# Expert 7 of the first part: single tiles between the experts of the second part, in place of one group of three ahead of the last

## The chip, the cores and the metric

The kernel runs on one core of one Trainium2 chip. Its time is the device time in microseconds (us); of several runs the median is given. Before the change it is 1835.74 us, the median of three runs between 1833.97 and 1839.69.

The core has a matrix engine (PE, whose weight loads are listed as PEld), a vector engine (DVE), a scalar engine (ACT), a general engine (POOL) and a queue engine that only issues transfers (SP). Transfers (DMAs) are issued by SP and by POOL, and run on 16 DMA engines that both share.

## The reference

Four layers follow one another on `x` of shape 16 x 256 x 256, all in 32-bit floats: a cross-attention with eight heads, a feed-forward layer with per-batch weight terms, a second cross-attention, and a mixture of eight experts. Only the last one matters here (cut; `_routing_weights` gives each token a weight for each expert, zero for most):

```python
def _L1_ffn_ref(x, Wg, Wu, Wd, Wr, temperature):
    weights = _routing_weights(x, Wr, temperature)
    gate = jnp.einsum('btd,edi->beti', x, Wg)
    up = jnp.einsum('btd,edi->beti', x, Wu)
    h = jax.nn.silu(gate) * up
    e_out = jnp.einsum('beti,eid->betd', h, Wd)
    out = jnp.einsum('bte,betd->btd', weights, e_out)
    return out
...
x = x + _L1_ffn_ref(_layernorm(x, axis=-1), L1_ffn_Wg, L1_ffn_Wu, L1_ffn_Wd, L1_ffn_Wr, L1_ffn_temperature)
```

Each of the eight experts has 256 inputs, 256 hidden values and 256 outputs. A token's output is the sum over the experts of weight times expert output, added to the token's `x`.

## The kernel before

**Attention and routing.** The main loop runs over 16 batches times 8 heads. Beside it, jobs in a list called `line` fill the gaps of PE: for every batch a job `chain` (the layers up to the second attention) and a job `route`. `route` works out the routing weights and writes each token's row (256 normalised values, eight weights and the token's number, `ROW` is 265 floats) into a slot of each expert that serves it. The slots lie in device memory, in `slots_d`, one array for each of two parts: the first part is batches 0 to 9 (`PARTS = (10, 6)`), the second is batches 10 to 15. The write is an indirect DMA issued by POOL (line 720), 16 for a batch. An expert's slots of the first part that are worked on are ten tiles of 128 rows, of the second part six tiles (`CAPS`).

**Experts.** The job `experts` works through a list of groups `G`. A group is one to four consecutive tiles of one expert and one part. For a group:

- `load` (line 1139) brings its rows from `slots_d` into a buffer `rows`, of which there are two. A read of a part's slots waits until all writes into this part have landed.
- `send_rows` transposes the rows in blocks of 32 on DVE (`to_blocks`, line 291) and sends them to device memory, the "hop" (line 296). `fetch_rows` copies token numbers and weights into `at` and `wt` (`take`, lines 1155 and 1158, six buffers each) and brings the hop back transposed, as `yTd` (`from_blocks`, line 302), in four DMAs. `yTd` has two buffers. All of these DMAs are issued by SP, in the order of the program.
- `gate` and `up` run, for each of two halves `i` of the hidden values, the products `pg` and `pu` over the group's tokens; ACT takes tanh (line 1202), DVE forms `sg` and `hTd` (lines 1212, 1213).
- `down` runs the products `pd` for one tile; DVE scales them by the weight (`o`, line 1228) and POOL adds the rows to `out` by an indirect DMA with addition (line 1229). The down products of a group are put into the program between the gate and up products of the next group.

All matrix products are recorded at line 80, in the helper `mm`. Their outputs share six PSUM buffers (`mm_tile`).

While group n is in work, group n+1 is ready, group n+2 is sent (at `i` = 0) and fetched (at `i` = 1), and the rows of group n+3 are loaded (at `i` = 0). A group of the second part isn't loaded before the routing job of the last batch has been written into the program (`ready`).

**Order of the additions.** Two additions to the same row of `out` must not overlap. `apart` declares that the scatters of one expert and part don't touch each other, and that a scatter of one part doesn't touch those of the other part. So the first scatter of an expert waits until the scatters of the expert before it, in the same part, have landed; scatters of the other part may be issued meanwhile.

**The list.** `groups(part, "", sizes)` makes the groups of each expert with the given numbers of tiles. The list before is: all groups of the first part (4, 3 and 3 tiles for each of experts 0 to 7) but the very last, then experts 0 to 6 of the second part (3 and 3), then the left-out group of expert 7 of the first part (3 tiles), then expert 7 of the second part (3, 2, 1). That makes 41 groups. The weights of an expert, once loaded, stay on the chip.

Of the kernel before, what the change touches and what calls it, by code (L numbers as in the profile page):

```python
# [29 lines left out]
def xattn_ffn_kernel(  # L30
# [16 lines left out]
    E = Wg.shape[0]  # L47
# [692 lines left out]
    with ExitStack() as sh, ExitStack() as sa, ExitStack() as sf:  # L740
# [545 lines left out]
        def groups(part, more, sizes, experts_=range(E)):  # L1286

            gs = []
            for e in experts_:
                t = CAPS[part] // P if more else 0  # L1290
                for k in sizes:
                    gs.append(G(part, e, t, k, more))
                    t += k
                assert t == NTOKS[part] // P if more else t == CAPS[part] // P
            return gs

        first = groups(0, "", (4, 3, 3))
        lists = (  # L1300
            first[:-1] + groups(1, "", (3, 3), range(E - 1))
            + first[-1:] + groups(1, "", (3, 2, 1), [E - 1])
        )

        last = None
        for n in range(NS + 2):
# [102 lines left out]
```

## Time and profile before

| What | Value |
|---|---|
| median of three runs | 1835.74 us |
| time of the profiled execution | 1834.93 us |
| its span | 1833.2 us |
| PE busy | 1805.1 us (98%) |
| DVE busy | 1211.1 us (66%) |
| POOL busy | 850.3 us (46%) |
| ACT busy | 583.9 us (32%) |
| DMA, mean over the span | 181 GB/s |
| granted PE clock, whole run | 0.996 |
| scatters into `out`, line 1229 | 128, mean 1562 ns |

The span is the time from the first to the last instruction of the program in the profiled execution. Busy times are averages over very different stages: in the attention stage POOL is little used, in the last 170 us it is used 60 to 80%. A row of the timeline gives the start of an instruction, its duration, and in brackets the idle time of its engine before it and what ended it. "PE busy" counts a modelled end of each product, and products overlap; the pace of the stage is better read from the starts in the chain of work. DMA rows named SPq are the issues on SP's queue: their duration is that of the issue, not of the transfer.

### The profile page before, as it was taken

The page shows a single profiled execution, that of the slowest core. Times are in us where ns is not written, and L with a number is a line of the kernel's source. Part 1 is how long each engine was busy: PE and PEld are TensorE (multiplying, and loading weights), DVE is VectorE, ACT ScalarE, POOL GpSimd, SP SyncE. Part 2 cuts the span into 40 slices and gives each one's busy share as a digit, 9 for nine tenths or more (in the row PEclk, how much of TensorE's full clock was granted, in tenths as well). Part 3 has the DMA queues.
Part 4 walks back from the last instruction along what each step waited for, and adds up shares of the span by engine and source line. Part 5 has one row for each costly group of instructions (what it writes and reads, how often), then busy time and mean ns, then how long its engine had stood idle before and what let it go on. Part 6 is the DMA issues. An engine that isn't in the chain of part 4 may idle for free.

```text
span 1833.2 us, 22646 instructions
## 1 busy us (share of the span) xinstructions
PE 1805.1 (98%) x6600; PEld 1228.8 (67%) x6600; DVE 1211.1 (66%) x3340; ACT 583.9 (32%) x1299; POOL 850.3 (46%) x988
## 2 busy tenths in 40 slices
PE   8999999999999999999999999999999999999996
PEld 4566666666676666666666666667666777666664
DVE  5456585858585858585858585858575676655553
ACT  3443433333333333334343434333333321111110
POOL 2122235353535353535353535353525267766665
PEclk9999999999999999999999999999999999999998
DMA  6553546464646464646464546554636577999996
GB/s 222 177 184 124 170 138 208 148 197 153 208 149 200 157 203 153 203 149 211 149 204 153 199 156 198 162 196 162 194 125 204 161 215 188 250 246 218 214 211 100
DMA packets 271181, 332.72 MB, mean 181 GB/s; under 512 B 31388, under 2 KB 222792, under 8 KB 271048
## 3 DMA queue, kind: packets, MB, share of 16 engines
q1 hardware_dynamic: 240280, 279.63, 48.4%
q0 software_dynamic: 30720, 51.54, 12.1%
q8 instruction: 55, 0.90, 0.2%
q14 instruction: 78, 0.64, 0.1%
q10 hardware_dynamic: 48, 0.01, 0.0%
HBM read 165.77 MB, written 165.28 MB: 181 GB/s over the span
## 4 chain that ended last, share of the span: by engine, by line
PE 94%; DMA 2%; DVE 2%; POOL 1%; issue 1%; SPq 0%; ACT 0%; DVEq 0%; POOLq 0%; ACTq 0%
PE po L80 13%; PE pv L80 13%; PE sc L80 13%; PE pk L80 12%; PE pq L80 7%; PE px L80 6%; PE pf L80 6%; PE ph L80 6%; PE pg L80 5%; PE pd L80 5%; PE pu L80 5%; PE pl L80 1%; DMA yTd<-hop_rows_b 1%; DMA rows<-slots_d 0%; DVE tb L912 0%
## 5 line engine op out<-in xcount | busy, mean ns | idle before, releaser
L904 POOL TENSOR_SCALAR pr<-pr,ri 128x512 f32<-128x512 f32 x256 | 179.1, 710 | 322.9 <-DVE ri L903 317.9
L896 ACT ACTIVATE pr<-sc,nm 128x512 f32<-128x512 f32 x256 | 173.6, 683 | 478.1 <-DVE nm L890 405.1
L720 POOL DMA_INDIRECT slots_d<-row,at_slot x256 | 253.2, 989 | 70.5 <-issue 69.4
L80 PE MATMUL po<-pT,v 128*128 128x256 f32 x1024 | 242.1, 379 | 1.8 <-DVE W2T L957 1.0
L1229 POOL DMA_INDIRECT out_dram<-o,at x128 | 200.0, 1562 | 92.8 <-issue 23.7
L80 PE MATMUL sc<-kT,qT 128*128 128x512 f32 x512 | 241.0, 593 | 1.5 <-ACT kT L829 1.5
L80 PE MATMUL pk<-kvT,Wk_sb 128*128 128x512 f32 x512 | 240.6, 592 | 0.0
L80 PEld LDWEIGHTS po<-pT,v 128*128 128x128 f32 x1024 | 194.2, 190 | 68.9 <-issue 36.0
L80 PE MATMUL pv<-Wv_sb,kvT 128*128 128x512 f32 x512 | 235.0, 592 | 0.0
L942 DVE TENSOR_SCALAR outT<-po,cvec 128x256 f32<-128x256 f32 x128 | 61.1, 477 | 246.4 <-PE po L80 233.1
L912 DVE STREAM_TRANSPOSE tb<-pr 128x512 f32<-128x512 f32 x256 | 165.8, 686 | 9.2 <-issue 5.0
L80 PEld LDWEIGHTS pv<-Wv_sb,kvT 128*128 128x128 f32 x512 | 97.0, 190 | 108.2 <-issue 103.1
L890 DVE TENSOR_REDUCE nm<-sc 128x1 f32<-128x512 f32 x256 | 160.3, 663 | 2.0 <-PE sc L80 1.9
L80 PEld LDWEIGHTS sc<-kT,qT 128*128 128x128 f32 x512 | 97.0, 190 | 69.9 <-issue 61.2
L80 PEld LDWEIGHTS pk<-kvT,Wk_sb 128*128 128x128 f32 x512 | 97.3, 190 | 67.8 <-issue 61.2
L80 PE MATMUL pq<-kvT,Wq_sb 128*128 128x256 f32 x512 | 133.0, 382 | 0.0
L1202 ACT ACTIVATE sg<-pg 128x384 f32<-128x384 f32 (+3 forms) x82 | 41.3, 503 | 281.3 <-PE pg L80 249.8
L80 PE MATMUL pg<-yTd,wx 128*128 128x384 f32 (+3 forms) x328 | 123.8, 500 | 1.2 <-DMA yTd<-hop_rows_b 0.9
L80 PEld LDWEIGHTS pq<-kvT,Wq_sb 128*128 128x128 f32 x512 | 96.5, 191 | 41.8 <-issue 28.2
L80 PE MATMUL pd<-wx,hTd 128*128 128x256 f32 x512 | 123.9, 379 | 0.2 <-DVE hTd L1213 0.2
L80 PE MATMUL pu<-yTd,wx 128*128 128x384 f32 (+3 forms) x328 | 123.6, 499 | 0.0
L80 PE MATMUL px<-Wo_sb,outT 128*128 128x256 f32 x512 | 121.8, 381 | 0.0
(205 smaller groups left out, 2652.4 us busy)
## 6 DMA issues: line engine op xcount, KB each, us to landing
hop<-tb SPq DMA_DIRECT2D x128, 512.0 KB
pT<-hop SPq DMA_DIRECT2D x512, 128.0 KB
ev<-ev_d SPq DMA_DIRECT2D x32, 512.0 KB
rows<-slots_d SPq DMA_DIRECT2D x31, 397.5 KB
hop_rows_b<-rows_b SPq DMA_DIRECT2D x30, 384.0 KB
yTd<-hop_rows_b SPq DMA_DIRECT2D x120, 96.0 KB
rows<-slots_d SPq DMA_DIRECT2D x8, 530.0 KB
cin<-in_ctx_dram SPq DMA_DIRECT2D x16, 256.0 KB
```

The costliest lines, as they stand in the source:

```text
L80: nc.tensor.matmul(out, lhsT, rhs, **kw)
L720: ins = nc.gpsimd.indirect_dma_start(out=slots_d[part], out_offset=bass.IndirectOffsetOnAxis(ap=at_slot[:, c, e : e + 1], axis=0), in_=row ...
L890: nc.vector.tensor_reduce(nm, sc, AX.X, ALU.max, negate=True)
L896: nc.scalar.activation(pr, sc, AF.Exp, bias=nm, accum_out=sm)
L904: nc.gpsimd.tensor_scalar(pr, pr, ri, 1.0, ALU.mult, ALU.mult)
L912: nc.vector.transpose(tb[:, :, c, :], heads[n][c][0].rearrange("p (m f) -> p m f", m=QP))
L942: nc.vector.tensor_scalar(o, po, col("bv", h), None, ALU.add)
L1202: nc.scalar.activation(self.sg, self.pg, AF.Tanh, scale=0.5)
L1229: ins = nc.gpsimd.indirect_dma_start(out=out_rows[0 : sum(NTOKS[: self.part + 1]), :], out_offset=bass.IndirectOffsetOnAxis(ap=self.at[:, ...
```

## The change

The first part's groups of expert 7 are cut as 3, 1, 1, 1, 1, 1, 1, 1 instead of 4, 3, 3. Its group of three stays behind expert 6 of the first part. The seven single tiles go one by one behind experts 0 to 6 of the second part. Expert 7 of the second part (3, 2, 1) ends the list, as before. The list now has 46 groups; the tiles are the same.

```diff
-        first = groups(0, "", (4, 3, 3))
-        lists = (
-            first[:-1] + groups(1, "", (3, 3), range(E - 1))
-            + first[-1:] + groups(1, "", (3, 2, 1), [E - 1])
-        )
+        first = groups(0, "", (4, 3, 3), range(E - 1)) + groups(0, "", (3,) + (1,) * 7, [E - 1])
+        lists = first[: 1 - E]
+        for e in range(E):
+            lists += groups(1, "", (3, 3) if e < E - 1 else (3, 2, 1), [e])
+            lists += first[1 - E :][e : e + 1]
```

In terms of the last boundary, one tile of the first part now stands ahead of expert 7 of the second part, where three stood. The second part begins after 22 groups instead of 23.

## Prediction

> **What bounds the kernel now.** I read the windows of 20 us over the last stage first, then the chain that ended last, then the engines' timelines there. The windows give busy time of PE, weight loads, DVE, ACT and POOL, the granted clock, the DMA engines' share and GB/s:
>
> ```profile
> 1720.00:1740.00 20.00, 20.00 (x73) 13.67 (x72) 11.84 (x31) 2.45 (x5) 11.98 (x8) 1.00 0.92 212
> 1740.00:1760.00 20.00, 20.00 (x74) 13.85 (x74) 12.40 (x34) 2.46 (x5) 14.25 (x10) 1.00 0.95 199
> ...
> 1800.00:1820.00 20.00, 17.41 (x81) 13.67 (x79) 10.24 (x27) 2.30 (x6) 16.83 (x11) 0.98 0.72 94
> 1820.00:1834.00 14.00, 0.00 (x0) 0.00 (x0) 0.00 (x0) 0.00 (x0) 3.23 (x3) 0.50 0.29 35
> ```
>
> PE never idles until 1817.6, and the DMA engines are over 90% taken. The chain (start, us, work) gives the pace:
>
> ```profile
> 1690.47 1.29 PE pg L80 x4
> 1691.76 1.29 PE pu L80 x4
> 1693.05 1.73 PE pd L80 x8
> 1694.78 1.29 PE pg L80 x4
> ...
> 1812.76 0.44 PE pg L80 x4
> 1813.21 0.45 PE pu L80 x4
> ```
>
> A group of three tiles takes 4 x 1.29 us for gate and up and 3 x 0.86 for the down products of the group before it, 7.75 us, and its successors start at 1698.22, 1705.97, 1713.72, without a hole. The last two lines are the only one-tile group of now. POOL is the other limit. Its timeline (start, us, then idle time before it):
>
> ```profile
> 1728.92 1.54 POOL L1229 DMA_INDIRECT out_dram<-o,at  x1 [0.30 <-issue]
> 1730.77 1.54 POOL L1229 DMA_INDIRECT out_dram<-o,at  x1 [0.31 <-issue]
> 1736.98 1.54 POOL L1229 DMA_INDIRECT out_dram<-o,at  x1 [4.66 <-DVE wt L1158]
> ...
> 1820.45 1.54 POOL L1229 DMA_INDIRECT out_dram<-o,at  x1 [0.30 <-issue]
> 1822.30 1.54 POOL L1229 DMA_INDIRECT out_dram<-o,at  x1 [0.30 <-issue]
> ```
>
> One scatter takes 1.85 us with its gap. Where the next expert of the same part begins, POOL stands 3.1 to 4.7 us: the DVE instruction named had long been done, so it is the landing of the expert before (start to next start is 4.7 to 6.2 us, mean 5.7). Six tiles are 13.9 to 15.5 us on POOL, mean 15.0, against 2 x 7.75 = 15.5 on PE, so POOL hardly catches up: expert 7's first scatter of the first part runs at 1693.85, 17 us after its tile was made, and the last one at 1822.30, 4.2 us after its tile (DVE's last o, 1817.64 to 1818.12). PE and POOL both bound the end, 4 us apart.
>
> **The change.** Tiles, weights, matmul columns and scatters stay the same in number; 41 groups become 46 (expert 7's 4, 3, 3 become 3 and seven ones). Added are 5 row loads, 5 hops and 20 fetches on SP's queue, and five sets of small DVE and ACT instructions.
>
> *PE work.* One-tile gate and up batches take 0.44 to 0.45 us, and a third of 1.29 is 0.43: 7 x 4 x 0.015 = 0.4 us. Against this stands the Trainium skill, "TensorE: Matmul & The Clock Gate", Back-to-back issue gap: in streams of weight load and matmul it measured about 81 ns at 128 columns and 131 at 512, so a short one costs 0.62 of a long one. Scaled to the 0.43 us of a 512-column instruction here (1.72 for four) this estimate is 0.27 us each, 7 x 16 x 0.16 = +18 us. The row is of the same operation in the same stage: I take 0.4.
>
> *POOL.* A single tile of expert 7 may scatter while the second part's landing is awaited: the groups are declared independent, and the crossing from one part to the other shows only 0.30 us of gap at 1706.78. From one boundary to the next POOL still needs 5 x 1.85 + 5.7 = 15.0 us, now for seven tiles, while PE needs 7 x 2.585 = 18.1. Started at 1693.85, it has worked off its lag by the sixth list. The six last scatters then follow their tiles: with o made at 1809.35, 1810.21, 1812.80, 1814.56, 1815.42 and 1817.64, the last starts at 1818.65 instead of 1822.30: **-3.65 us**. More cannot come, since PE's last product stands in front. From here every stall of PE counts in full.
>
> *The start of the second part.* It moves one group of four tiles forward. Its first rows are loaded one group earlier, where SP now issues another row load at 1652.02. But the last scatter into the slots is issued by POOL at 1653.69, and its semaphore reaches its last count at 1659.44. SP stands 7.4 us with the fetch of expert 7's tiles behind it (now at 1657.01; then about 1660.0 to 1661.7, landing near 1665.9 instead of 1664.28): PE +1.5. The rows land 5 to 7 us after 1659.5; DVE's transposes, now at 1659.28, wait in line until about 1665.5, with the o, sg and hTd behind them; the hop leaves at 1666.7, lands at 1670.5, the fetch lands at 1675.5. The second part could have begun at 1664.41 + 7.75 = 1672.16: **+3.4 us**, between 0 (rows landing at once, six PSUM buffers covering DVE) and 6.
>
> *Index buffers.* `at` has six buffers, freed by the landing of scatters six groups back; DVE already waits twice for that, 2.6 us each. Six groups now span 2 x 18.1 = 36 us rather than 46.5, with POOL late. Going through the takes with the start shifted by 3.4, two meet a wait of 1.7 us while PE has PSUM buffers to fill: 0.3, from 0 to 3.
>
> *The prefetch at short groups.* SP's order for a group is hop, next row load, four fetches; a fetch waits for the hop's landing:
>
> ```profile
> 1694.68 0.34 SPq L296 DMA_DIRECT2D hop_rows_b<-rows_b  x1
> 1695.07 0.43 SPq L1139 DMA_DIRECT2D rows<-slots_d  x1
> 1697.78 1.74 SPq L302 DMA_DIRECT2D yTd<-hop_rows_b  x4
> ```
>
> The hop is issued 4.21 us after its group's first gate (1690.47). I took the landings from the semaphores: in the thirteen groups from here to 1790, hop issue to the last fetch's landing took 6.97 to 9.58 us, mean 8.4 (five early ones 9.0, eight later ones 8.0). The data are needed two groups on, 15.5 us after the first gate: 2.9 us spare. Now the groups are 7.75 (second of a list), 4.3 (4 x 0.43 + 3 x 0.86, a single) and 6.0 (first of a list, one down product). A list's first group has 7.75 + 4.3 - 4.21 = 7.86 us: put against the thirteen times, the excess is 0.62 on the mean. Its second group is sent from within the single, about 2.5 us in (1.47 to hTd, 1.05 for three transposes), its rows some 0.35 late, and is needed at 4.3 + 6.0 + 0.6: 2.85 + 8.4 - 10.95 = 0.3, with the spread 0.5. Seven times 0.62 and six times 0.5 are **+7.3 us**. The single itself has some 3.7 us to spare.
>
> Here the skill's price differs: "DMA: Bandwidth & Descriptors", Anatomy of one DMA, sets about 2.0 us plus bytes at 436 GB/s. That makes the hop 2.9 us and the fetch 1.3 of issue plus 2.2, 6.4 in all, under 7.86: no stall, and a sum of about zero. It was fitted for the other issuing path, and the trace's 8.4 was taken with the engines 92 to 95% shared. The trace decides; 0 and 16 us (all at 9.5) are kept as ends.
>
> **Sum** against the profiled execution, 1834.93 us (span 1833.2 and 1.7 around it): 0.4 + 3.4 + 0.3 + 7.3 - 3.65 = +7.75, or 1842.7. The median of the runs, 1835.74, is 0.8 higher, which gives 1843.5; I trim half a microsecond for the relief that stalls give to the DMA engines: **1843 us**.
>
> **Rivals.** (1) *The prefetch keeps up*: landings near 8 us throughout; then 0.4 + 3.4 + 0 to 1 - 3.65, about 1836, and 1832.5 where the start costs nothing either. For it speaks that the later landings are 8.0; against it that even these exceed 7.86. It decides where PE's stalls sum to less than 3.65. This is the case that ends not slower. (2) *Contention grows*: while it works off its lag POOL issues a scatter each 2.14 us instead of 2.5, on engines already over 0.92 taken. At 9.5 us the two stalls are 1.65 and 0.6 in each round: 7 x 2.25 = 16, or 1852. (3) *The single does not pass the wait*: if POOL waited before and after it, a round would be 7 x 1.85 + 2 x 3.9 = 20.7 us where PE has 18.1; the last list would start near 1699.4 + 7 x 20.7 = 1844.3 instead of 1813.05, the end near 1867; the 0.30 at the crossings speaks against it. (4) *Faster by over 0.3%* would need 5.5 us (about what a measurement of this kernel can tell from no change): only 3.65, and 0.95 of an old PE stall at 1664.41, are in sight.
>
> **How the numbers follow.** The forecast 0.50 (its own range 1838 to 1848), (1) 0.27, (2) 0.17, (3) 0.02, (4) 0.04. Slower by over 0.3% is above 1841.2: 0.40 of the forecast's 0.50, (2) and (3), 0.59. Same: 0.10 and most of (1), 0.35. Faster 0.06. The range holds (1) without its start-free end and (2) up to a little beyond its price: 1834 to 1855.
>
> **What would show it.** Right: POOL's gaps at the second part's boundaries near 2 us early and its scatters following their tiles at the end; PE holes before pg, ended by the yTd fetch, at lists' first and second groups, some 1 us a round; SP waiting some 7 us for the slots; PE's last product about 11 us later. Wrong: a gapless PE in the second part, or DVE waits at `at` or `rows` that stop PE for longer than the fetches do.

## The result

The changed kernel takes 1847.63 us (median of four runs, 1846.85 to 1849.13), the kernel before 1837.72 us in the same comparison (1833.97 to 1840.48). The ratio is 1.006, with a 95% interval from 1.0044 to 1.0076: slower by 8 to 14 us. The forecast was 1843 us in 1834 to 1855, and slower with a chance of 0.59. Direction and mechanism came as forecast; the loss is 9.9 us by the medians, where 7.3 were forecast (1843 less the 1835.74 of the kernel before).

The windows of the last stage of the changed kernel (stretch, its length, busy time of PE, weight loads, DVE, ACT and POOL with the numbers of instructions, granted clock, DMA share, GB/s; a packet counts whole in the window where it starts, so a share can pass 1):

```profile
1720.00:1740.00 20.00, 16.91 (x71) 11.81 (x70) 9.70 (x30) 2.52 (x6) 15.62 (x11) 1.00 1.01 206
1740.00:1760.00 20.00, 18.61 (x78) 13.01 (x77) 11.34 (x33) 2.52 (x6) 11.86 (x8) 1.00 0.85 190
...
1820.00:1840.00 20.00, 11.84 (x59) 9.41 (x57) 7.38 (x21) 1.48 (x5) 9.94 (x7) 0.94 0.54 72
```

PE was busy for the whole of the first two windows before the change (20.00 in both, in the prediction's first lines); now it lacks 3.1 and 1.4 us. Its own timeline shows where (start, duration, and in brackets the idle time before and what ended it):

```profile
1723.62 1.53 PE L80 MATMUL pg<-yTd,wx 128*128 128x384 f32 x4 [1.55 <-DMA yTd<-hop_rows_b]
...
1731.44 0.61 PE L80 MATMUL pg<-yTd,wx 128*128 128x128 f32 x4
1731.89 0.61 PE L80 MATMUL pu<-yTd,wx 128*128 128x128 f32 x4
1732.34 1.89 PE L80 MATMUL pd<-wx,hTd 128*128 128x256 f32 x8
...
1737.52 1.53 PE L80 MATMUL pg<-yTd,wx 128*128 128x384 f32 x4 [1.54 <-DMA yTd<-hop_rows_b]
```

The single tile itself starts on time at 1731.44, and its batches follow one another in 0.45 us. The holes stand ahead of groups of three on both sides of a single, and the fetch of their transposed rows ends them. POOL's timeline shows the other side:

```profile
1727.89 1.54 POOL L1229 DMA_INDIRECT out_dram<-o,at  x1 [0.30 <-DMA out_dram<-o,at]
1730.87 1.54 POOL L1229 DMA_INDIRECT out_dram<-o,at  x1 [1.44 <-DVE sg L1212]
...
1749.20 1.54 POOL L1229 DMA_INDIRECT out_dram<-o,at  x1 [5.65 <-DVE o L1228]
...
1832.90 1.54 POOL L1229 DMA_INDIRECT out_dram<-o,at  x1 [0.30 <-issue]
1834.75 1.54 POOL L1229 DMA_INDIRECT out_dram<-o,at  x1 [0.30 <-issue]
```

The scatter at 1727.89 is the single's. Behind it, at the boundary of 1730.87, POOL stands 1.44 us instead of some 4: the single's scatter fills the rest, as the change intends. From 1749.20 on, in expert 3 of the second part, POOL has caught up and waits for tiles (DVE's `o`). Its last scatter starts 1.23 us after its tile is ready (DVE ends it at 1833.52), instead of 4.17.

For each profile I took three lengths, all from starts and ends in the timelines: from expert 6's first gate product in the first part to PE's last down product; from the last tile on DVE to POOL's last scatter; and from that scatter's end to the end of the span.

| Kernel | PE, expert 6 to its last product | last tile to last scatter | rest |
|---|---|---|---|
| before | 180.20 us (1637.41 to 1817.61) | 4.17 | 9.37 |
| changed | 193.15 us (1639.85 to 1833.00) | 1.23 | 9.77 |

The spans differ by 12.9 us: +12.95 on PE, -2.94 on POOL's lag, +0.4 at the end, and 2.4 before expert 6, where the two programs are the same and executions spread. The change proper is +10.4 us in this pair of profiles. "Holes" below are delays between the starts of two batches on PE, beyond the pace of the batch ahead (0.43, 0.32, 0.22 and 0.11 us for an instruction of 512, 384, 256 and 128 columns). A "round" is one expert of the second part with the single behind it. Counted so from 1690 on, the rounds of the changed kernel hold 9.6 us of holes in this profile (the expectations below put it at 9.9). Of the 12.95 us on PE, 9.6 are these holes and 2.0 the start of the second part; the rest is many small delays, such as 0.08 us in the batch behind each hole.

### The profile page after: what moved, and what is told of

It reads as the page before. It is cut to its first block, busy times and chain, and to the rows that moved or that the text cites. A ratio compares the mean times of both kernels' runs of the same rounds, so it can differ in the third digit from the quotient of the medians.

```text
span 1846.1 us, 22919 instructions
## 1 busy us (share of the span) xinstructions
PE 1809.4 (98%) x6680; PEld 1234.4 (67%) x6680; DVE 1213.9 (66%) x3370; ACT 585.9 (32%) x1309; POOL 852.8 (46%) x988
## 4 chain that ended last, share of the span: by engine, by line
PE 89%; DMA 5%; DVE 2%; POOL 1%; issue 1%; SPq 1%; ACT 0%; ACTq 0%; POOLq 0%; DVEq 0%
PE po L80 13%; PE pv L80 13%; PE sc L80 13%; PE pk L80 11%; PE pq L80 7%; PE px L80 6%; PE pf L80 6%; PE ph L80 6%; PE pg L80 4%; PE pu L80 4%; PE pd L80 3%; DMA yTd<-hop_rows_b 2%; POOL out_dram L1229 1%; DMA rows<-slots_d 1%; PE pl L80 1%
## 5 line engine op out<-in xcount | busy, mean ns | idle before, releaser
L80 PEld LDWEIGHTS po<-pT,v 128*128 128x128 f32 x1024 | 194.1, 190 | 69.4 <-issue 35.9
```

The costliest lines, as they stand in the source:

```text
L80: nc.tensor.matmul(out, lhsT, rhs, **kw)
```

## The experiments

The theory at this point: a group next to a single tile has a shorter window between the issue of its hop and its use; hop and fetch take about as long as that window, because the DMA engines are shared with POOL's scatters; so PE waits. The rivals to this: the start of the second part costs most of it, the waits for the `at` buffers do, or small groups cost by their number.

### A smaller dose

```diff
-        first = groups(0, "", (4, 3, 3), range(E - 1)) + groups(0, "", (3,) + (1,) * 7, [E - 1])
-        lists = first[: 1 - E]
+        first = groups(0, "", (4, 3, 3), range(E - 1)) + groups(0, "", (4, 3, 1, 1, 1), [E - 1])
+        lists = first[:-3]
...
-            lists += first[1 - E :][e : e + 1]
+            if 4 <= e < E - 1:
+                lists += first[-3:][e - 4 : e - 3]
```

> A smaller dose: expert 7 of the first part as 4, 3, 1, 1, 1, the 4 and the 3 in front of the second part, the three singles behind its experts 4, 5 and 6. If each round with a single costs PE some 1.4 us, three cost 4.2 us, the start of the second part costs nothing, and POOL's last scatter follows its tile by about 1 us instead of 4.2: 1 to 2 us above the kernel before, 8 us under the changed kernel. If the loss comes mostly from the start of the second part or from the number of groups as such, it is not in proportion: within 2 us of the kernel before with no holes, or as slow as the changed kernel.

The ratio to the kernel before is 1.000 (0.9988 to 1.0013), where the changed kernel, timed on the same chip, has 1.0049 (1.0029 to 1.0069). All holes of PE in the second part:

```profile
1763.33 1.53 PE L80 MATMUL pg<-yTd,wx 128*128 128x384 f32 x4 [0.83 <-DMA yTd<-hop_rows_b]
1782.85 1.53 PE L80 MATMUL pg<-yTd,wx 128*128 128x384 f32 x4 [1.13 <-DMA yTd<-hop_rows_b]
1790.48 1.53 PE L80 MATMUL pg<-yTd,wx 128*128 128x384 f32 x4 [1.38 <-DMA yTd<-hop_rows_b]
1803.19 1.53 PE L80 MATMUL pg<-yTd,wx 128*128 128x384 f32 x4 [0.34 <-issue]
```

They appear only where the singles stand, and sum to 4.35 us beyond the pace, 1.45 for each single; seven in the changed kernel made 9.6. PE's stretch is 183.77 us, 3.6 above the kernel before, and POOL's lag is 1.22 us, 2.95 less: nearly even, as timed. The loss grows with the number of singles, and three suffice for all of POOL's gain.

### Nothing in between

```diff
-        first = groups(0, "", (4, 3, 3), range(E - 1)) + groups(0, "", (3,) + (1,) * 7, [E - 1])
-        lists = first[: 1 - E]
-        for e in range(E):
-            lists += groups(1, "", (3, 3) if e < E - 1 else (3, 2, 1), [e])
-            lists += first[1 - E :][e : e + 1]
+        lists = (
+            groups(0, "", (4, 3, 3)) + groups(1, "", (3, 3), range(E - 1))
+            + groups(1, "", (3, 2, 1), [E - 1])
+        )
```

> All groups of the first part come first (4, 3, 3 for every expert), then the second part without anything between its experts. The forecast's view of POOL: PE's holes stay near 1 us as before, but the last expert's first scatter has to wait for the landing of expert 6, some 4 us more on POOL, and POOL's last scatter sets the end: last scatter about 8 us behind its tile instead of 4.2, time about 4 us above the kernel before. If PE alone sets the end, the time is that of the kernel before within 1 us.

POOL's end in this kernel:

```profile
1814.91 1.54 POOL L1229 DMA_INDIRECT out_dram<-o,at  x1 [0.30 <-issue]
1819.53 1.54 POOL L1229 DMA_INDIRECT out_dram<-o,at  x1 [3.08 <-DVE hTd L1213]
...
1828.77 1.54 POOL L1229 DMA_INDIRECT out_dram<-o,at  x1 [0.30 <-issue]
```

The wait of the last boundary (3.08 us) stands ahead of expert 7's six scatters, and the last of them starts 8.64 us after its tile, as expected (about 8). PE has no hole in the second part, and its stretch is 179.20 us. The time is less clear: the ratio is 1.0004 (0.9992 to 1.0015), 0.9 us by the medians and at most 2.8 us above the kernel before, where 4 was expected. In the profile the lag's 4.5 us are cut by 1.0 us of shorter PE stretch and 0.3 us of shorter rest. So the lag is shown, but its price in the time is smaller than I had put it, or hidden in the spread; by the times alone, "PE alone sets the end" is not excluded.

### The engines without the scatters

```diff
+                if self.part == 1:
+                    return
                 ins = nc.gpsimd.indirect_dma_start(
```

> The changed kernel, but the scatters of the second part into the output are left out, so its output lacks the experts' part for batches 10 to 15; matrix products, loads, hops and fetches are all there. If the fetch's landings are late because the DMA engines are shared with the scatters, hop to last landing falls from some 8.4 to about 7 us, under the 7.86 us window, and the holes of PE in the rounds of the second part fall from 9.9 us to 2 or less. If the chain of hop and fetch is too long by itself, or SP's order makes it late, 7 us or more of the holes stay.

The stretch of 70 us in the middle of the second part, first of the changed kernel, then of this one (columns as above):

```profile
1720.00:1790.00 70.00, 64.66 (x259) 44.70 (x258) 38.59 (x109) 9.03 (x21) 41.91 (x29) 1.00 0.88 194
```

```profile
1720.00:1790.00 70.00, 69.41 (x295) 50.59 (x294) 43.20 (x126) 9.57 (x23) 4.63 (x3) 1.00 0.60 160
```

With the share of the DMA engines at 0.60 instead of 0.88, PE is busy 69.4 of 70 us, with the same list of groups. The rounds keep 1.3 us of holes out of 9.6. By the semaphores, the time from the issue of a hop to the last landing of its fetch is 6.4 us on the mean in the rounds (after the scatters of the first part have ended), against 8.1 in the changed kernel and 8.4 in the kernel before. (The 6.4 and 8.1 are means over groups of three and singles together.) The window of a list's first group is 7.86 us. So neither the number of groups, nor SP's order, nor the length of the chain by itself makes the holes: the chain fits without the scatters, and does not when they share the engines. Whether the scatters hinder it in the engines or in the memory behind them, the run can't tell, since it takes away both loads. It also takes away the waits for buffers that a scatter frees; of these DVE has one of 2.0 us from 1690 on in the changed kernel, and the run with nine such buffers (below) keeps its holes. PE's stretch is 182.74 us, 2.5 above the kernel before, which bounds everything else that the short groups cost. The time, 0.9962 of the kernel before (0.9949 to 0.9975), is no comparison, as 48 scatters are missing.

### A deeper prefetch

The hop is sent three groups ahead from group 23 on, with a third buffer for the rows; the fetch stays two ahead (cut: `load`, which takes the third buffer).

```diff
-                    if n + 2 < len(groups):
-                        if i == 0:
-                            groups[n + 2].send_rows()
-                        else:
-                            groups[n + 2].fetch_rows()
-                    if i == 0 and n + 3 < len(groups):
-                        groups[n + 3].load()
+                    if i == 0:
+                        ahead_ = 3 if n >= 23 and ready is not None else 2
+                        while sent_to <= min(n + ahead_, len(groups) - 1):
+                            groups[sent_to].send_rows()
+                            sent_to += 1
+                            if sent_to < len(groups):
+                                groups[sent_to].load(
+                                    D_.more if n >= 23 and sent_to % 3 == 2 else None
+                                )
+                    elif n + 2 < len(groups):
+                        groups[n + 2].fetch_rows()
```

> The changed kernel with the hop sent three groups ahead instead of two from group 23 on, rows loaded four ahead into a third buffer; the fetch stays two ahead. The fetch then no longer waits for a hop issued in the same group. If the short window between hop and use makes the holes, those of the rounds fall from 9.9 us to about 1.5 (one of them where the deeper order begins), and the time falls by about 8 us, to 2 us above the kernel before. If the holes come from something else in short groups (SP's number of issues, PE's queue), they stay and the time is that of the changed kernel.

The ratio is 1.0036 (1.0025 to 1.0047), 6.6 us above the kernel before by the medians, where 2 were expected: little is gained. The holes of the rounds do fall, to some 4 us, but the group where the deeper order begins loads and sends at once. DVE there:

```profile
1685.90 1.09 DVE L291 STREAM_TRANSPOSE rows_b<-rows 128x256 f32<-128x256 f32 x3
1692.62 1.10 DVE L291 STREAM_TRANSPOSE rows_b<-rows 128x256 f32<-128x256 f32 x3 [5.62 <-DMA rows<-slots_d]
```

DVE stands 5.62 us for rows just asked for, and PE has a hole of 3.3 us. Behind it another 1.9 us go, almost without idle time: PE runs at a granted clock of 0.50 there (the last section comes back to this). Rows late by a little also remained the wait of the rounds (from 1640 on DVE waits 22.2 us for rows in eleven places; 9.8 in five in the changed kernel). The second version loads the rows two groups ahead of their hop, starts that one group earlier, and copies token numbers and weights with the hop (with nine buffers; cut: everything but the new order):

```diff
+                        deep = n >= 23 and ready is not None
+                        while sent_to <= min(n + (3 if deep else 2), len(groups) - 1):
+                            groups[sent_to].send_rows(deep)
+                            sent_to += 1
+                        far = 5 if deep else 4 if n == 22 and ready is not None else 3
+                        while loaded_to <= min(n + far, len(groups) - 1):
+                            groups[loaded_to].load(
+                                D_.more if n >= 22 and loaded_to % 3 == 2 else None
+                            )
+                            loaded_to += 1
```

> The changed kernel with the hop sent three groups ahead from group 23 on, as in the deeper run before, but the rows loaded two groups ahead of their hop (started one group earlier, so that no group loads and sends at once), token numbers and weights copied with the hop, and nine buffers for them. If the rows' lateness made what was left of the holes in the deeper run, the hole of some 5 us at its start goes and the rounds have 2 us or less in all: about 9 us under the changed kernel, within 2 us of the kernel before, and POOL's last scatter within 2 us of its tile. If the shared DMA engines set the rate themselves, the holes stay near the 4 us that the deeper run's rounds had.

The ratio is 1.0028 (1.0017 to 1.0038), some 4 us under the changed kernel in the same comparison (1.0049) and short of the 9 expected, so late rows were not the whole cause. The second groups of the lists have no holes any more. The first groups keep 0.25 to 1.9 us each, 5.2 in all, and SP's waits in this kernel say why (engine and line, what it waited for: us in total, times, longest):

```profile
SPq L296 <- DVE o L1243: 62.1, 21, 7.0
SPq L302 <- PE pu L80: 23.4, 18, 4.9
...
SPq L302 <- DMA hop_rows_b<-rows_b: 7.4, 4, 2.2
```

The fetch hardly waits for the hop any more (7.4 us, where the same view of the changed kernel has 66.8); it now waits for PE's last up product of the group whose `yTd` buffer it takes, one of two. From there the first group has 0.86 us of down product and 4.3 us of the single, 5.2 us, for a fetch that took 5.0 to 6.8 us in the five groups that waited, by the semaphores. One window is only exchanged for the next. A third `yTd` buffer would have to follow; it wasn't tried. The start of the deeper order still costs a hole of 3.25 us, and 1.4 us behind it that I had not counted (see the last section).

### The start of the second part

First, one single in front of the second part, so that this part begins at group 23 as before:

```diff
-        lists = first[: 1 - E]
+        lists = first[: 2 - E]
         for e in range(E):
...
-            lists += first[1 - E :][e : e + 1]
+            if e > 0:
+                lists += first[2 - E :][e - 1 : e]
```

> The changed kernel with the first single moved in front of the second part, behind expert 7's group of three, so that the second part begins at group 23 again, as before the change, and one round fewer has a single. If SP's stand at the slots costs PE 2 us, SP waits there 1 us or less instead of 6.2, the hole of 1.84 us at the second part's second group goes, and with one round less (1.4) the time is about 3 us under the changed kernel. If that hole has another cause, the time falls by no more than 1.4 us.

SP's stand at the slots is gone, but the ratio is 1.0043 (1.0033 to 1.0053), no gain beyond the one round less, and the profile (one of the slowest executions, 1853.07 us against a median of 1847.24) has a new wait on DVE, in the same place:

```profile
1684.00 0.41 DVE L1155 CAST at<-rows 128x3 uint32<-128x3 f32 x1 [5.59 <-DMA out_dram<-o,at]
```

With a single so early, six groups span less time than POOL's lag, and DVE waits for an `at` buffer. PE has a hole of 2.25 us behind it and then loses another 1.8 at a granted clock of 0.50. As a test of the start it failed: one wait took the place of the other. So the slots' writes were moved instead, in the changed kernel:

```diff
-                    yield 2.6 if b < B - 2 else 5.2
+                    yield 2.6
```

> The changed kernel with the last two batches' slot writes spaced by 2.6 in the plan instead of 5.2, so that POOL writes them some 10 us earlier. If SP's stand at the slots costs PE the hole at the start of the second part, the stand goes (it was 6.2 us) and with it 2 us of the time; the holes of the rounds stay at 9 to 12 us. If POOL's lag grows instead, the waits for token-number buffers take the place of what is gained and the time stays.

SP's stand goes, and PE's stretch is 191.14 us, 2.0 us shorter than in the changed kernel, as expected from this part; the rounds keep 10.5 us of holes. But the time does not fall: the ratio is 1.0077 (1.0063 to 1.0091), above both of the changed kernel (1.006 and 1.0049), though the intervals overlap. The loss lies 100 us earlier, which the last experiment shows.

### The waits for `at`

```diff
-                self.at = D_.wk.tile([P, TG], U32, tag="at", bufs=6, name=f"at_{self.name}")
+                self.at = D_.wk.tile([P, TG], U32, tag="at", bufs=9, name=f"at_{self.name}")
...
-                self.wt = D_.wk.tile([P, TG], F32, tag="wt", bufs=6, name=f"wt_{self.name}")
+                self.wt = D_.wk.tile([P, TG], F32, tag="wt", bufs=9, name=f"wt_{self.name}")
```

> The changed kernel with nine buffers instead of six for token numbers and weights. DVE waited there 6 us in one profile of the changed kernel and 10 in the other. If these waits are hidden behind PE's filled PSUM buffers, as forecast (0.3 us), the waits go and the time stays within 1.5 us of the changed kernel, holes in the rounds 9 to 12 us. If they make holes by holding back the transposes, the holes fall by 3 us or more and so does the time.

The waits are gone, and the ratio is 1.0054 (1.004 to 1.0068), beside 1.006 and 1.0049 for the changed kernel in its two comparisons: no gain to be seen. PE's stretch of 192.10 us is 1.0 and 1.5 below the two profiles of the changed kernel (193.15 and 193.55); the holes from 1690 on sum to 10.0 us. So the holes of the rounds do not come from these waits. What the waits cost is 1 to 1.5 us by the stretches, which themselves differ by 0.4 between two profiles of one kernel; the times, with intervals 5 us wide, can't confirm it.

The changed kernel was timed again among these runs:

> The changed kernel itself, timed beside the next three on one chip so that they can be set against it: 9 to 11 us (0.5 to 0.6%) above the kernel before, with 9 to 11 us of holes of PE in the rounds.

1.0049 (1.0029 to 1.0069); its holes in the rounds sum to 12.1 us.

### The same aim with groups of three

```diff
-        first = groups(0, "", (4, 3, 3), range(E - 1)) + groups(0, "", (3,) + (1,) * 7, [E - 1])
-        lists = first[: 1 - E]
-        for e in range(E):
-            lists += groups(1, "", (3, 3) if e < E - 1 else (3, 2, 1), [e])
-            lists += first[1 - E :][e : e + 1]
+        first = groups(0, "", (4, 3, 3))
+        lists = (
+            first[:-2] + groups(1, "", (3, 3), range(3))
+            + first[-2:-1] + groups(1, "", (3, 3), range(3, E - 1))
+            + first[-1:] + groups(1, "", (3, 2, 1), [E - 1])
+        )
```

> The change's aim without short groups: expert 7 of the first part keeps 4, 3, 3, with the 4 in front of the second part, one 3 behind its expert 2 and one 3 behind expert 6, so two waits for a landing are covered and every window of the prefetch keeps some 11 us. If short groups make the holes, there are none in the rounds; SP stands at the slots and PE loses up to 2 us at the start of the second part; POOL's last scatter follows its tile by 1 to 2 us instead of 4.2: from 2 us under the kernel before to 1 us above it. If any list of the first part between experts disturbs the prefetch, holes of 1 us or more stand at these two places.

PE has no hole in the rounds, POOL's lag is 1.22 us, and SP stood 5.5 us at the slots: lists of the first part between experts do no harm where the groups stay long. What is left is the start of the second part, where this kernel has a hole of 2.3 us and then a slow stretch; the sum of both is 4.1 us. The ratio is 0.9993 (0.9981 to 1.0006), no difference from the kernel before that can be told. With the slots written earlier (the edit above), and then with nine buffers as well:

> The version with groups of three (4 in front, 3 behind expert 2, 3 behind expert 6) and the slots written earlier. Its start cost 4.1 us of holes, of which part was PE at a lower granted clock behind a pause. If SP's stand makes them, they fall to about 1 us, and the time is 4 to 5 us (0.2 to 0.27%) under the kernel before: 3.65 us from POOL's end and 1 us from an old hole. If something else is late at this place, it stays 1 us under the kernel before.

> The same with nine buffers for token numbers and weights as well. If earlier slot writes raise POOL's lag so that these buffers stop DVE, this version is 1 to 3 us faster than the one with six; if not, the two agree within 1 us.

Both have 1.0009 (1.0001 to 1.0018 and 1.0 to 1.0018): not faster, and the 4 to 5 us expected are missed. The two agree, so the buffers make no difference here. The start's holes shrink as expected, to 0.9 us and to none (PE's stretch is 179.90 and 179.07 us, where the version with late slots has 183.11). But PE now waits at the last batch's attention layer. PE of the version with late slots, then PE, DVE and POOL of the first of the two with early slots, all from around 1540 us:

```profile
1539.39 0.87 PE L84 MATMUL ycT_p<-ident,yc 128*128 128x128 f32 x4 [0.58 <-DVE yc L267]
```

```profile
1543.44 1.22 PE L84 MATMUL ycT_p<-ident,yc 128*128 128x128 f32 x4 [5.05 <-DVE yc L267]
```

```profile
1542.98 0.74 DVE L267 TENSOR_SCALAR yc<-x,mv_q,rs_q 128x256 f32<-128x256 f32 x2 [5.36 <-POOL rs_q L262]
```

```profile
1538.36 0.97 POOL L720 DMA_INDIRECT slots_d<-row,at_slot  x1 [0.30 <-issue]
1539.63 0.96 POOL L720 DMA_INDIRECT slots_d<-row,at_slot  x1 [0.30 <-issue]
1540.90 0.96 POOL L720 DMA_INDIRECT slots_d<-row,at_slot  x1 [0.31 <-issue]
1541.89 0.25 POOL L261 TENSOR_SCALAR rs_q<-mv_q 128x2 f32<-128x2 f32 x1
```

The slot writes moved forward now stand on POOL ahead of the two small instructions that the layer norm of the last batch needs, and PE waits 5 us for it (5.34 in the version with nine buffers). In the changed kernel with early slots PE waits 5.32 us for the same instructions, so its time went there too. In these three profiles expert 6 of the first part begins at 1642.3 to 1644.5; in the profiles of the kernel before and of the changed one it was 1637.4 to 1639.9. Early slots pay back what they gain; none of the versions is shown to be faster than the kernel before.

## Why the prediction was right, point by point

- **PE work, 0.4 us: held.** One-tile batches take 0.44 to 0.45 us, as the single group at the end had shown. The estimate from the Trainium skill's ratio of small to large products ("TensorE: Matmul & The Clock Gate", Back-to-back issue gap) was 18 us; the run without scatters leaves 2.5 us on PE for everything but the sharing, its remaining holes included.
- **POOL, -3.65 us: right in kind, a little less in size.** The lag at the end fell from 4.17 to 1.23 us, 2.94. The other 0.7 is a misreading of the trace: the forecast lets the last six scatters start with the first of the `o` times that it lists, 1809.35, but these are DVE's starts. That `o` ends at 1809.83 and a scatter follows 0.28 later; with 1.85 for each of the next five the last starts at 1819.36, 2.94 us sooner than 1822.30. (The 17 us of lag at 1693.85 are 15.2 by the trace.) POOL worked off its lag by the fourth list, not the sixth. The size in the time is less sure, since a lag raised by 4.5 us showed as at most 2.8.
- **Start of the second part, +3.4 us: too high.** SP stood 6.2 us (7.4 forecast) and DVE waited 4.1 and 2.8 us for the rows, so the chain was right. But PE's holes there were 1.26 us (1.11 before) and 1.84 in one profile of the changed kernel, 2.0 us more than before, and 0.97 and none in the other, nothing more. The late fetch for expert 7 cost next to nothing, not 1.5. The second part's first group, ahead of which the 3.4 us were placed, came without a hole in both; its hop and fetch took 7.7 and 8.0 us, not the 8.8 worked out. The 1.84 stands ahead of the second group, whose hop and fetch took 9.9 us (7.3 in the other profile). With the slots early the stretch is 2.0 to 2.4 us shorter.
- **Index buffers, +0.3 us: small, as forecast,** 1 to 1.5 us by the stretch in the run with nine buffers, near the limit of what can be told.
- **The prefetch at short groups, +7.3 us: the right mechanism, mis-sized.** First groups: 4.5 us in seven, where seven times 0.62 were forecast. Second groups: 5.1 us in seven, where six times 0.5 were forecast. Their mean was 0.72, and the last list's group of two counts as well (1.12), which I had left out. Their hop and fetch took 8.5 us on the mean (8.9 in the second profile), not 8.4, and their windows were 7.1 to 9.0 us where one of 8.1 was assumed. The sum is 9.6 us in one profile and 12.1 in the other. The run without scatters shows the sharing as the condition, the smaller dose and the groups of three show the short group as the other.
- **The skill's price against the trace.** The estimate from "DMA: Bandwidth & Descriptors", Anatomy of one DMA, was 6.4 us for hop and fetch together, the trace's 8.4. The run without scatters gives 6.4 us: the page's figure fits this kernel with the engines 0.60 busy, and the 8.4 was the right one for this stage. The difference of 2 us decides whether a loss was to be forecast at all.
- **Rivals.** Prefetch in time (1) would have needed the engines free. Contention that grows (2) is there, but small: the mean of 8.1 holds the singles, whose hop is a third as large. Groups of three alone, from 1730 to 1790, took 8.4 and 8.5 us in the two profiles of the changed kernel, against 8.0 before; the rival had 9.5. The single does pass the wait (3): its scatters start 0.3 us behind those of the second part.

In sum the misses have opposite signs: 2 to 5 us too little for the rounds and 0.7 too much gained on POOL, against 1 to 3 too much for the start. That the total came as near as it did is in part luck; the direction is not, since the rounds alone cost more than POOL had to give.

## What to carry to other kernels

A prefetch that runs a fixed number of groups ahead has a window in time that shrinks with the group: before cutting work into smaller pieces, add up the durations of the groups between issue and use, and set them against the measured time from issue to landing in that stage, under its own DMA load. Filling a wait on an engine is worth only its lag at the end where another engine is as close to the bound: here 4.2 us on POOL against PE without a hole, of which 2.9 could be had: every version that fills the wait ends with some 1.2 us, because the last six scatters follow one another at 1.85 us. And each cure moved the wait to the next buffer or the next instruction on the same queue, so what stands behind a moved instruction is to be counted first.

## What was not expected of the hardware

A pause of PE of 2 us or more can cost more than its own length. In the even deeper version PE paused for 3.1 us up to 1695.81; the granted clock (third column from the end) then fell:

```profile
1692.00:1694.00 2.00, 0.73 (x4) 0.30 (x2) 1.31 (x5) 0.00 (x0) 0.00 (x0) 1.00 1.19 263
1694.00:1696.00 2.00, 0.19 (x1) 0.22 (x2) 0.00 (x0) 0.00 (x0) 0.22 (x1) 0.82 1.10 321
1696.00:1698.00 2.00, 2.00 (x4) 1.09 (x5) 0.00 (x0) 0.00 (x0) 1.70 (x2) 0.50 0.88 137
1698.00:1700.00 2.00, 2.00 (x7) 1.17 (x6) 0.56 (x1) 0.49 (x1) 1.70 (x2) 0.83 0.65 80
```

The next four products of 384 columns took 2.69 us to the next batch instead of 1.29, another 1.4 us. The lines add up to some 3.4 us at a clock of 0.50, and the other traces show the same: behind a pause of 3.13 us in the deeper version, of 2.16 in the version with groups of three (1.8 us of the 4.1 lost there), of 2.08 with one single in front (1.8 us), and of 5.05 with early slots (in the other two versions with early slots it begins within the pause of 5.3 us and lasts twice as long).

The length of the pause alone does not decide it. In the second profile of the changed kernel PE paused 2.10 us up to 1715.38, in the changed kernel with early slots 2.06 us up to 1740.21, and the clock stayed at 1.00. What makes the difference between 2.08 and 2.10 us, these runs don't show. In both profiles of the changed kernel it stayed at 1.00 from 1690 to 1820, through all holes of the rounds, so this took no part in its loss.

The Trainium skill warns of such pauses ("TensorE: Matmul & The Clock Gate", Why this matters for your kernels: none over about 3 us). The pauses of 3.1 and 5.05 us agree with it; those of 2.08 and 2.16 us had the same after them and are shorter.
